# Two graph layers on Trainium2: bank reads of pass 2 ahead of other ready work, and the second tile's softmax and end placed half a pair later

## Chip, core and metric

The kernel runs on one core of one Trainium2 chip. The metric is the device time in microseconds (us) of the whole program. Everything is float32 on the way in and out.

## What is computed

Two layers over 128 graphs of 64 nodes with 768 features. Each layer normalizes its input, clips it at zero, computes a graph layer and adds it to its input. The first graph layer (pass 1 of the kernel) multiplies by three 768x768 weights and mixes by the adjacency. The second (pass 2) is a gated graph attention with six heads of 128. Cut to the second:

```python
def _L1_gnn_ref(feat_in, adj, W, b, w_src, w_dst, H_w, H_b):
    h = jnp.einsum('bni,hio->bhno', feat_in, W)
    th = jnp.tanh(h)
    attn_src = jnp.einsum('bhno,hoz->bhnz', th, w_src)
    attn_dst = jnp.einsum('bhno,hoz->bhnz', th, w_dst)
    attn = attn_src + jnp.swapaxes(attn_dst, -1, -2)
    attn = jnp.where(attn >= 0, attn, leaky_alpha * attn)
    attn = jnp.where(mask, NEG_MASK, attn)          # mask: adj == 0
    attn = jax.nn.softmax(attn, axis=-1)
    feat_out = jnp.einsum('bhnm,bhmo->bhno', attn, h) + b
    feat_out = jax.nn.elu(...)                       # heads side by side
    gate = jax.nn.sigmoid(feat_in @ H_w.T + H_b)
    return gate * feat_out + (1.0 - gate) * feat_in

h = jnp.maximum(_layernorm(x, axis=-1), 0.0)
x = x + _L1_gnn_ref(h, adj, ...)
```

## The kernel before

A tile is 128 rows, that is two graphs; a pair is two tiles; there are 32 pairs, and each pass goes through them. In pass 2 the input of a pair (256 x 768) times the two weights (features W and gate H_w, side by side) is computed by a fast matrix scheme: the operand is cut into 2 x 3 blocks, the weights into 3 x 3, and 15 products of sums of blocks (f1 to f11 of the input, g of the weights) give the six blocks of the output instead of 18. The products go into four named banks of PSUM, a (two buffers), b, c and d (one each). A product after the first in a bank is added to what the bank holds, and each time the bank is read, the reading is added to or taken from one block of the output. So the next product into a bank has to wait until the last one was read.

```python
PRODUCTS = (   # input sum, weight sum, bank, first in the bank, output block, sign, ...
    ("f1", "g6", "a", True, "11", "+", False),
    ("f7", "g10", "b", True, "00", "-", False),
    ("a01", "b11", "d", True, "01", "+", True),
    ("f4", "b21", "a", False, "01", "-", False),
    ("a00", "g12", "b", False, "01", "-", False),
    ("f3", "g8", "c", True, "12", "-", False),
    ("a02", "g14", "a", False, "00", "-", False),
    ("f9", "g9", "b", False, "02", "+", False),
    ("f11", "b10", "d", True, "00", "+", True),
    ("f6", "g5", "a", False, "02", "+", False),
    ("f8", "g3", "b", False, "12", "-", False),
    ("f10", "b12", "c", False, "02", "+", True),
    ("f5", "b22", "a", False, "12", "-", False),
    ("a11", "g1", "b", False, "11", "+", True),
    ("f2", "g11", "a", False, "10", "+", True),
)
```

The reading of a bank and the product (line numbers as in the profile: L736 and L738 add or take away, L741 to L748 are the first writes of a block):

```python
def read(b, c, sign, first, ss):
    # ... to: block c of the output, ps: the bank
    op = nc.vector.tensor_add if sign == "+" else nc.vector.tensor_sub
    if not first:
        if sign == "+":
            op(to, ps, to)                     # L736
        else:
            op(to, to, ps)                     # L738
        return
    if ss.start == 0:
        nc.scalar.activation(to[:, 0], ps[:, 0], AF.Copy,           # L741
                             scale=1.0 if sign == "+" else -1.0)
    if ss.stop == 2:
        s = 1 - ss.start
        if sign == "+":
            op(to[:, s], ps[:, s], hbb[:, cols])                    # L746
        else:
            op(to[:, s], hbb[:, cols], ps[:, s])                    # L748

def product(an, bn, b, first, c, sign, begins, ss):
    def step(q):
        # ...
        nc.tensor.matmul(bank[b][:, : n * CQ], OPS[p, an][:, q, :],     # L755
                         bw2[bn][:, ...], start=(first and q == 0), stop=(q == KQ - 1), ...)
        if q == KQ - 1:
            read(b, c, sign, begins, ss)
    for q in range(KQ):
        steps.append(lambda q=q: step(q))

for ss in ((slice(0, 2),) if p < NP - 1 else (slice(0, 1), slice(1, 2))):
    # ... 15 products each: 30 steps of 512 columns, in the last pair 60 of 256
```

Around these products lies the work of the tiles, by these functions (cut):

```python
heads(t)    # ScalarE tanh (L774), VectorE product with w_src and w_dst (L776),
            # 12 ScalarE sums over a head (L781, L783), GpSimd splits them in bf16 (L784 to L791)
swap(t)     # DMA: the two graphs of the tile change halves
gate(t)     # ScalarE tanh of the gate (L811)
rows(t)     # TensorE (L803), VectorE (L805), ScalarE (L807): row factors of the scores
softmax(t)  # TensorE scores (L819), VectorE masks (L821), ScalarE leaky (L823),
            # VectorE maximum (L825), 6 ScalarE exponentials (L829)
turn_p(t)   # 3 TensorE transposes (L840), ScalarE copy (L842)
attend(t)   # 12 TensorE products (L857), 6 VectorE operations (L861)
final(t)    # ScalarE exponential (L871), VectorE L872, L873, L874, GpSimd starts the output DMA
turn, form  # TensorE transposes of the next pair's input (L704), ScalarE copies (L709),
            # VectorE sums f1 to f11 (L241, L243)
```

For each pair the steps of the products are merged with side work: each entry is placed ahead of the product step of its number. The order in which the entries are written down is the priority; a scheduler then orders each engine's instructions by priority and readiness, once, when the program is built. Each engine runs its own list in order.

```python
def behind(p):      # the tiles of the pair before, beside the products of this one
    t0, t1 = 2 * p, 2 * p + 1
    return [(0, lambda: gate(t0)),
            (1, lambda: (heads(t1), swap(t1))),
            # ... see the diff
            (22, lambda: final(t1))]

def last():         # the last pair's own tiles, beside its own products
    return [(31, lambda: (heads(t1), swap(t1))),
            # ...
            (38, lambda: rows(t0)), (40, lambda: softmax(t0)),
            (46, lambda: rows(t1)), (48, lambda: softmax(t1)),
            (54, lambda: turn_p(t0)), (56, lambda: attend(t0)),
            (99, lambda: gate(t0)), ...]                     # the rest after the products

for p in range(NP):
    more = [(3, lambda: finish(NP - 1))] if p == 0 else []
    if p == NP - 1:
        more += last()
    merged(main(p), own(p) + before(p + 1) + behind(p - 1) + more)
```

Of the kernel before, what the change touches and what calls it, by code (L numbers as in the profile page):

```python
# [79 lines left out]
def kernel(  # L80
# [56 lines left out]
    NP = NT // 2  # L137
# [501 lines left out]
    with ExitStack() as px:  # L639
# [16 lines left out]
        def load_x(t):  # L656
            p, k = divmod(t, 2)
            HM[t] = work.tile([P, D], F32, name="x", bufs=2)
            nc.sync.dma_start(HM[t], HHD[p][k * P : (k + 1) * P, :])
# [58 lines left out]
        def main(p):  # L718

            bank = {}  # L720
            steps = []
            for k in range(2):
                t = 2 * p + k
                HS[t] = hzs[t % 4][:, 0, :].rearrange("p (h o) -> p h o", h=H)
                Z[t] = hzs[t % 4][:, 1, :]

            def read(b, c, sign, first, ss):

                k, q = int(c[0]), int(c[1])
                cols = slice(q * CQ, (q + 1) * CQ)  # L730
                to = hzs[(2 * p + k) % 4][:, ss, cols]
                ps = bank[b][:, : (ss.stop - ss.start) * CQ].rearrange("p (s n) -> p s n", n=CQ)
# [19 lines that stand above are left out]
                    if first and q == 0:  # L752
                        bank[b] = psm.tile([P, 512], F32, name=f"pm{b}", bufs=2 if b == "a" else 1)
                    n = ss.stop - ss.start
                    nc.tensor.matmul(  # L755
                        bank[b][:, : n * CQ], OPS[p, an][:, q, :],
                        bw2[bn][:, (2 * q + ss.start) * CQ : (2 * q + ss.stop) * CQ],
                        start=(first and q == 0), stop=(q == KQ - 1), skip_group_check=True)
                    if q == KQ - 1:
                        read(b, c, sign, begins, ss)  # L760
                for q in range(KQ):
                    steps.append(lambda q=q: step(q))

            for ss in ((slice(0, 2),) if p < NP - 1 else (slice(0, 1), slice(1, 2))):
                seen = set()
                for an, bn, b, first, c, sign, _ in PRODUCTS:
                    product(an, bn, b, first, c, sign, c not in seen, ss)
                    seen.add(c)
            return steps

        def heads(t):

            th = work.tile([P, H, DO], F32, name="th")
            nc.scalar.activation(th, HS[t], AF.Tanh)  # L774
            pr = work.tile([P, 2, H, DO], F32, name="pr")
            nc.vector.tensor_mul(pr, th[:, None].to_broadcast([P, 2, H, DO]),  # L776
                                 wsd.rearrange("p s (h o) -> p s h o", h=H))
            sd = small.tile([P, 2, H], F32, name="sd")
            sg = small.tile([P, 3, H], F32, name="sg")
            for h in range(H):  # L780
                nc.scalar.activation(pr[:, 1, h, :], pr[:, 1, h, :], AF.Copy, accum_out=sd[:, 1, h : h + 1])  # L781
            for h in range(H):
                nc.scalar.activation(pr[:, 0, h, :], pr[:, 0, h, :], AF.Copy, accum_out=sg[:, 2, h : h + 1])  # L783
            nc.gpsimd.tensor_mul(sg[:, :GT, :], sd[:, 1:2, :].to_broadcast([P, GT, H]),  # L784
                                 gm[:, :, None].to_broadcast([P, GT, H]))
            sb = sdb[t % 2]
            for i in range(NPART):
                q = sb[:, :, i * H : (i + 1) * H]
                nc.gpsimd.tensor_copy(q, sg)
                if i < NPART - 1:  # L790
                    nc.gpsimd.tensor_sub(sg, sg, q)  # L791

        def swap(t):

            hx = HX[t] = work.tile([P, H, DO], F32, name="hx")
            for g in range(GT):
                nc.sync.dma_start(hx[g * N : (g + 1) * N], HS[t][(1 - g) * N : (2 - g) * N])

        def rows(t):


            ps = pss.tile([P, 512], F32, name="ps")
            nc.tensor.matmul(ps[:NR, : N + P], sdb[t % 2].rearrange("p c v -> p (c v)")[:, :NR], idr,  # L803
                             start=True, stop=True)
            nc.vector.tensor_mul(rrow[t % 2][: 2 * HB],  # L805
                                 ps[: 2 * HB, None, :N].to_broadcast([2 * HB, H, N]), de[: 2 * HB])
            nc.scalar.copy(lrow[t % 2][2 * HB :], ps[2 * HB : NR, N : N + P])  # L807

        def gate(t):

            nc.scalar.activation(Z[t], Z[t], AF.Tanh, scale=0.5)  # L811

        def softmax(t):

            p, k = divmod(t, 2)
            a = work.tile([P, H, N], F32, name="a")
            nc.gpsimd.memset(a, NEG_MASK / LEAKY)
            pl = pss.tile([P, 512], F32, name="ps")[:, : H * N].rearrange("p (h n) -> p h n", h=H)
            nc.tensor.matmul(pl, lrow[t % 2], rrow[t % 2], start=True, stop=True)  # L819

            nc.vector.copy_predicated(a, AI[p][:, k, None, :].to_broadcast([P, H, N]), pl)  # L821
            al = work.tile([P, H, N], F32, name="al", bufs=1)
            nc.scalar.activation(al, a, AF.Prelu, alpha=LEAKY)  # L823
            mx = small.tile([P, H], F32, name="mx")
            nc.vector.tensor_reduce(mx, al, AX.X, OP.max, negate=True)  # L825
            pb = PB[t] = work.tile([P, H, N], F32, name="pb")
            dn = DN[t] = small.tile([P, H], F32, name="dn")
            for h in range(H):
                nc.scalar.activation(pb[:, h, :], al[:, h, :], AF.Exp, bias=mx[:, h : h + 1],  # L829
                                     accum_out=dn[:, h : h + 1])  # L830
            nc.vector.reciprocal(dn, dn)
# [3 lines left out]
        def turn_p(t):  # L835

            pt = PT[t] = work.tile([P, HH, P], F32, name="pT")
            ps = pss.tile([P, 512], F32, name="ps")[:, : HH * P].rearrange("p (a b) -> p a b", a=HH)
            for c in range(HH):
                nc.tensor.transpose(ps[:, c, :],  # L840
                                    PB[t][:, 2 * c : 2 * c + 2, :].rearrange("p h n -> p (h n)"), ident)
            nc.scalar.copy(pt, ps)  # L842
# [55 lines left out]
        def behind(p):  # L898

            if p < 0:  # L900
                return []
            t0, t1 = 2 * p, 2 * p + 1
            return [(0, lambda: gate(t0)),
                    (1, lambda: (heads(t1), swap(t1))),
                    (2, lambda: load_x(t0)),
                    (4, lambda: gate(t1)),
                    (4, lambda: rows(t0)),
                    (6, lambda: softmax(t0)),
                    (10, lambda: load_x(t1)),
                    (11, lambda: rows(t1)),  # L910
                    (13, lambda: softmax(t1)),
                    (12, lambda: turn_p(t0)),
                    (14, lambda: attend(t0)),
                    (15, lambda: final(t0)),
                    (19, lambda: turn_p(t1)),
                    (21, lambda: attend(t1)),
                    (22, lambda: final(t1))]

        def last():

# [23 lines left out]
# [5 lines that stand above are left out]
# [45 lines left out]
```

## Time and profile before

| | |
|---|---|
| time, median of 3 | 2579.61 us (2579.23 to 2581.2) |
| span of the profiled execution | 2577.0 us, TensorE clock granted 0.993 |
| pass 1 | up to about 1510 us |
| pass 2 | from there to the end |
| a pair in the middle of pass 2 (2001.80 to 2034.07 us) | 32.27 us |
| in it busy: TensorE, VectorE, ScalarE, GpSimd | 31.25, 26.58, 22.51, 7.45 us |

A row of the waits names the engine and line that waited, and the engine and line that ended the wait. In the timeline the columns are the start, the length, the engine, the line, the operation and what it writes and reads, and how many instructions stand together in the row; a wait ahead of it is in square brackets. A float32 product of the kernel appears as two records. The ends of matmuls are modelled, so the pace of TensorE is read from the starts.

### The profile page before, as it was taken

The page shows a single profiled execution, that of the slowest core. Times are in us where ns is not written, and L with a number is a line of the kernel's source. Part 1 is how long each engine was busy: PE and PEld are TensorE (multiplying, and loading weights), DVE is VectorE, ACT ScalarE, POOL GpSimd, SP SyncE. Part 2 cuts the span into 40 slices and gives each one's busy share as a digit, 9 for nine tenths or more (in the row PEclk, how much of TensorE's full clock was granted, in tenths as well). Part 3 has the DMA queues.
Part 4 walks back from the last instruction along what each step waited for, and adds up shares of the span by engine and source line. Part 5 has one row for each costly group of instructions (what it writes and reads, how often), then busy time and mean ns, then how long its engine had stood idle before and what let it go on. Part 6 is the DMA issues. An engine that isn't in the chain of part 4 may idle for free.

```text
span 2577.0 us, 35545 instructions
## 1 busy us (share of the span) xinstructions
PE 2489.3 (97%) x12072; PEld 1714.2 (67%) x12072; DVE 1980.3 (77%) x4130; ACT 1079.5 (42%) x3588; POOL 492.3 (19%) x801
## 2 busy tenths in 40 slices
PE   5999999999999999999999999999999999999996
PEld 4788888888888888888888864444444444444444
DVE  8977777777777777777777557888888888888887
ACT  1222222222222122222222216666666666666666
POOL 0121121211212112121121111222222222222222
PEclk8999999999999999999999999999999999999998
DMA  5122121221312212122121263444444444444433
GB/s 172 56 74 80 52 102 52 76 78 52 103 52 76 78 52 102 52 78 76 52 101 50 79 203 78 100 100 100 99 100 100 101 100 101 99 100 100 100 75 77
DMA packets 115047, 224.19 MB, mean 87 GB/s; under 512 B 36538, under 2 KB 48941, under 8 KB 114866
## 3 DMA queue, kind: packets, MB, share of 16 engines
q1 hardware_dynamic: 105208, 196.70, 23.3%
q0 software_dynamic: 9504, 25.17, 6.9%
q8 instruction: 95, 1.56, 0.3%
q14 instruction: 86, 0.70, 0.1%
q10 hardware_dynamic: 154, 0.06, 0.0%
HBM read 95.67 MB, written 100.66 MB: 76 GB/s over the span
## 4 chain that ended last, share of the span: by engine, by line
PE 71%; DVE 18%; ACT 6%; issue 4%; DMA 1%; POOL 1%; SPq 0%; POOLq 0%; DVEq 0%; ACTq 0%
PE pwa L544 19%; PE pwb L544 16%; PE pwc L544 6%; PE pma L755 6%; PE pwd L544 6%; PE pmb L755 6%; PE pb L497 5%; DVE f L861 3%; ACT pb L829 3%; DVE op L243 3%; PE pmc L755 2%; DVE pr L776 2%; DVE f L874 2%; DVE f L872 2%; DVE weights L738 1%
## 5 line engine op out<-in xcount | busy, mean ns | idle before, releaser
L544 PE MATMUL pwa<-weights,op 128*128 128x256 f32 x2304 | 542.6, 383 | 4.3 <-DVE x L536 3.1
L544 PEld LDWEIGHTS pwa<-weights,op 128*128 128x128 f32 x2304 | 423.0, 190 | 73.4 <-DVE x L536 12.0
L243 DVE TENSOR_TENSOR op<-op 128x768 f32<-128x768 f32 (+1 forms) x512 | 339.8, 683 | 156.4 <-ACT op L505 154.5
L505 ACT COPY op<-pb 128x768 f32<-128x768 f32 x160 | 124.2, 798 | 757.0 <-PE pb L497 757.0
L755 PE MATMUL pma<-weights,op 128*128 128x512 f32 (+1 forms) x792 | 381.5, 597 | 35.2 <-DVE weights L738 29.3
L544 PE MATMUL pwb<-weights,op 128*128 128x256 f32 x1536 | 372.2, 383 | 12.9 <-DVE x L538 9.5
L544 PEld LDWEIGHTS pwb<-weights,op 128*128 128x128 f32 x1536 | 285.9, 191 | 60.7 <-DVE x L538 10.3
L755 PE MATMUL pmb<-weights,op 128*128 128x512 f32 (+1 forms) x528 | 252.4, 591 | 3.6 <-DVE weights L738 3.5
L755 PEld LDWEIGHTS pma<-weights,op 128*128 128x128 f32 x792 | 137.8, 191 | 173.8 <-issue 96.4
L225 POOL TENSOR_TENSOR rn<-ve,mhalf 128x1 f32<-128x1 f32 x128 | 89.0, 695 | 530.5 <-DVE ve L224 526.9
L544 PE MATMUL pwc<-weights,op 128*128 128x256 f32 x768 | 184.9, 383 | 0.0
L544 PE MATMUL pwd<-weights,op 128*128 128x256 f32 x768 | 176.2, 379 | 0.0
L755 PEld LDWEIGHTS pmb<-weights,op 128*128 128x128 f32 x528 | 97.0, 193 | 118.4 <-issue 82.9
L218 DVE BATCH_NORM_STATS2 st<-x 128x6 f32<-128x384 f32 x256 | 136.4, 547 | 44.7 <-DMA x<-in_x_dram 43.5
L476 POOL COPY c<-cnt 128x243 bf16<-128x243 bf16 x64 | 46.2, 751 | 649.3 <-PE pb L484 602.3
L497 PE MATMUL pb<-r,h 64*128 64x192 f32 x1536 | 153.0, 339 | 7.8 <-ACT h L406 7.7
L544 PEld LDWEIGHTS pwc<-weights,op 128*128 128x128 f32 x768 | 143.2, 190 | 25.1 <-issue 7.0
L544 PEld LDWEIGHTS pwd<-weights,op 128*128 128x128 f32 x768 | 145.9, 190 | 19.8
L572 ACT ACTIVATE hf<-x,rn 128x768 f32<-128x768 f32 x64 | 65.8, 1028 | 213.7 <-DVE rn L226 213.7
L497 PEld LDWEIGHTS pb<-r,h 64*128 64x128 f32 x1536 | 124.6, 189 | 42.7 <-issue 30.5
L829 ACT ACTIVATE pb<-al,mx 128x64 f32<-128x64 f32 x384 | 128.3, 335 | 14.8 <-DVE mx L825 14.8
L574 POOL TENSOR_TENSOR x<-x,hf 128x768 f32<-128x768 f32 x64 | 115.9, 1812 | 85.4 <-ACT hf L572 85.4
(152 smaller groups left out, 4160.3 us busy)
## 6 DMA issues: line engine op xcount, KB each, us to landing
x<-in_x_dram SPq DMA_DIRECT2D x64, 384.0 KB
h<-hf SPq DMA_DIRECT2D x64, 384.0 KB
out_dram<-x SPq DMA_DIRECT2D x64, 384.0 KB
hh<-hh SPq DMA_DIRECT2D x64, 384.0 KB
h<-h SPq DMA_DIRECT2D x64, 384.0 KB
x<-hh SPq DMA_DIRECT2D x64, 384.0 KB
hx<-weights SPq DMA_DIRECT2D x128, 192.0 KB
out_dram<-f POOLq DMA_DIRECT2D x62, 384.0 KB, 4.9
```

The costliest lines, as they stand in the source:

```text
L218: ins = nc.vector.bn_stats(st[:, i, :], src[:, i * HALF : (i + 1) * HALF])
L225: nc.gpsimd.tensor_tensor(to[:, 0:1], ve, mhalf, op=OP.pow)
L243: return (nc.vector.tensor_add if s1 == "+" else nc.vector.tensor_sub)(to, x, y)
L497: nc.tensor.matmul(ps[:, g, i * 3 * N : (i + 1) * 3 * N], H0[t][s, kb * P : (kb + 1) * P], rts[p % 2][s, k].rearrange("p s n -> p (s n)"), ...
L505: nc.scalar.copy(a.rearrange("p h s (g n) -> p g (h s) n", g=GT), ps[:, :, : 6 * N].rearrange("p g (x n) -> p g x n", n=N))
L544: nc.tensor.matmul(bank[b][:, :CQ], OPS[p, an][:, q, s, :], bw[bn][:, (s * KQ + q) * CQ : (s * KQ + q + 1) * CQ], start=(first and q == s ...
L572: nc.scalar.activation(h, X[t], AF.Relu, scale=to[:, 0:1], bias=to[:, 1:2])
L574: nc.gpsimd.tensor_add(X[t], X[t], h)
L755: nc.tensor.matmul(bank[b][:, : n * CQ], OPS[p, an][:, q, :], bw2[bn][:, (2 * q + ss.start) * CQ : (2 * q + ss.stop) * CQ], start=(first a ...
L776: nc.vector.tensor_mul(pr, th[:, None].to_broadcast([P, 2, H, DO]), wsd.rearrange("p s (h o) -> p s h o", h=H))
L829: nc.scalar.activation(pb[:, h, :], al[:, h, :], AF.Exp, bias=mx[:, h : h + 1], accum_out=dn[:, h : h + 1])
L861: nc.vector.scalar_tensor_tensor(FF[t][:, h * DO : (h + 1) * DO], po[h % 2][:, h // 2, :], DN[t][:, h : h + 1], bb, op0=OP.mult, op1=OP.add)
```

## The change

Two things. First, the reads of pass 2's banks are put down under high priority, so that the scheduler takes a read that is ready before any other ready work of its engine. Second, the side work of the pair before is placed anew: the second tile's softmax, attention and end come some half a pair (about 15 steps) after the first tile's, instead of closely behind. Beside the last pair, which has 60 steps in place of 30, the numbers are doubled. What it is for: the next product into a bank shall not wait because its read stands behind end operations on VectorE, and the two tiles' work on VectorE and ScalarE shall be spread over the pair.

```diff
--- before.py
+++ after.py
@@ -757,7 +757,8 @@
                         bw2[bn][:, (2 * q + ss.start) * CQ : (2 * q + ss.stop) * CQ],
                         start=(first and q == 0), stop=(q == KQ - 1), skip_group_check=True)
                     if q == KQ - 1:
-                        read(b, c, sign, begins, ss)
+                        with tc.high_priority():
+                            read(b, c, sign, begins, ss)
                 for q in range(KQ):
                     steps.append(lambda q=q: step(q))
 
@@ -900,21 +901,23 @@
             if p < 0:
                 return []
             t0, t1 = 2 * p, 2 * p + 1
-            return [(0, lambda: gate(t0)),
-                    (1, lambda: (heads(t1), swap(t1))),
-                    (2, lambda: load_x(t0)),
-                    (4, lambda: gate(t1)),
-                    (4, lambda: rows(t0)),
-                    (6, lambda: softmax(t0)),
-                    (10, lambda: load_x(t1)),
-                    (11, lambda: rows(t1)),
-                    (13, lambda: softmax(t1)),
-                    (12, lambda: turn_p(t0)),
-                    (14, lambda: attend(t0)),
-                    (15, lambda: final(t0)),
-                    (19, lambda: turn_p(t1)),
-                    (21, lambda: attend(t1)),
-                    (22, lambda: final(t1))]
+            steps = [(0, lambda: gate(t0)),
+                     (2, lambda: load_x(t0)),
+                     (4, lambda: rows(t0)),
+                     (6, lambda: softmax(t0)),
+                     (6, lambda: (heads(t1), swap(t1))),
+                     (8, lambda: gate(t1)),
+                     (12, lambda: turn_p(t0)),
+                     (14, lambda: attend(t0)),
+                     (15, lambda: final(t0)),
+                     (15, lambda: load_x(t1)),
+                     (16, lambda: rows(t1)),
+                     (18, lambda: softmax(t1)),
+                     (24, lambda: turn_p(t1)),
+                     (26, lambda: attend(t1)),
+                     (27, lambda: final(t1))]
+
+            return [(2 * i, f) for i, f in steps] if p == NP - 2 else steps
 
         def last():
```

## Prediction

> **What bounds the kernel now.** I read the page's busy shares and slices first, to see how many stages there are, then the waits of TensorE alone, then one pair of tiles of pass 2 in the timeline, then the stretches of the tail.
>
> ```profile
> PE 2489.3 (97%) x12072; PEld 1714.2 (67%) x12072; DVE 1980.3 (77%) x4130; ACT 1079.5 (42%) x3588; POOL 492.3 (19%) x801
> PE   5999999999999999999999999999999999999996
> PEld 4788888888888888888888864444444444444444
> DVE  8977777777777777777777557888888888888887
> ACT  1222222222222122222222216666666666666666
> ```
>
> Two stages show. Up to about 1510 us is pass 1; from there pass 2, in which the weight loads fall from 8 to 4 tenths, VectorE rises to 8 and ScalarE to 6. Only pass 2 is touched by the change. TensorE is "busy" nearly everywhere, so what counts is who it waits for:
>
> ```profile
> PE pma L755 <- DVE weights L738: 29.3, 29, 1.0
> PE pwb L544 <- DVE x L538: 9.5, 2, 8.7
> PE pb L497 <- ACT h L406: 7.7, 1, 7.7
> PE pb L443 <- DVE ab L415: 4.5, 1, 4.5
> PE pmb L755 <- DVE weights L738: 3.5, 1, 3.5
> ```
>
> The columns are total us, number of waits, longest. One wait comes back 29 times, 1.0 us each: a product into bank a cannot start until VectorE has read that bank (line 738). Pass 2 has 32 pairs, so this is once in nearly every pair. The timeline of TensorE and then of VectorE around one of them:
>
> ```profile
> 1993.22 1.98 PE L755 MATMUL pma<-weights,op 128*128 128x512 f32 x4
> 1995.04 1.02 PE L755 MATMUL pmb<-weights,oq 128*128 128x512 f32 x2
> ...
> 1998.91 1.88 PE L755 MATMUL pmd<-weights,op 128*128 128x512 f32 x4
> 2001.80 0.70 PE L755 MATMUL pma<-weights,op 128*128 128x512 f32 x1 [1.01 <-DVE weights L738]
> ```
> ```profile
> 1995.80 1.74 DVE L776 TENSOR_TENSOR pr<-th,wsd 128x1536 f32<-128x1536 f32 x1
> 1997.46 0.95 DVE L872 SCALAR_TENSOR_TENSOR f<-e,f 128x768 f32<-128x768 f32 x1
> ...
> 1999.87 0.95 DVE L874 SCALAR_TENSOR_TENSOR f<-weights,f 128x768 f32<-128x768 f32 x1
> 2000.74 0.41 DVE L243 TENSOR_TENSOR op<-op 128x256 f32<-128x256 f32 x1
> 2001.07 0.68 DVE L738 TENSOR_TENSOR weights<-weights,pma 128x512 f32<-128x512 f32 x1
> ```
>
> The product f5·b22 leaves bank a at about 1995.04. Its read runs at 2001.07, six us later, because VectorE first does the score product (L776), the three end operations of the second tile (L872 to L874) and three sums of operands. TensorE fills in with the next pair's f1 and a01 products and then stands still for f2·g11. The pmd group starts at 1998.91; four records of 512 columns advance 1.72 us elsewhere (1995.04 to 1995.89 is two of them), so the next group could start at 2000.63 and starts at 2001.80: 1.17 us lost. The pair repeats every 32.27 us (2001.80 to 2034.07).
>
> How much of 32.27 us is work? By starts: 30 products of 0.86 us = 25.8; 12 transposes of the operands, 0.108 each = 1.3; 6 of the probabilities = 0.65; two groups of 12 small attention products, 0.89 each = 1.8; the row and score products of two tiles, about 0.5. Sum 30.1 us. So 2.2 us are lost: 1.17 in the bubble, about 1.0 in some ten places of 0.1 us, where a weight load is released just too late (after the copy of the probabilities, after each attention group, after row factors from GpSimd or ScalarE).
>
> **The Trainium skill.** "Perfetto Trace Analysis", section Identifying the Most-Contended Engine, says that matmul busy time is no measure of closeness to the limit and that weight-load busy time is better. The trace agrees: 97% busy, yet 2.2 of 32.27 us per pair (7%) can be won. The same page, section Optimization Strategy, says that a bubble that repeats on the engine that should be saturated can mean too few buffers. Here the trace shows another cause: the bank's reader is queued behind unrelated work. "PSUM — Partial Sum Buffer", section Engine vs sequencer instructions, says that VectorE's and ScalarE's queues are strictly first in, first out. The trace agrees: the L738 read could have run from 1995.04 but ran in its place in the order, after L874.
>
> **The change, part by part.** No instruction is added or removed; the counts per pair stay (80 on TensorE, 54 on VectorE, 60 on ScalarE). What moves is the order that the scheduler makes.
>
> 1. Reads first. In the changed order the f5 read stands directly behind L776 and ahead of the operand sums; no end operation stands between. I walk one pair with the durations above, with t = 0 at the end of f10·b12 (bank c). TensorE: four transposes 0.43, f5 to 2.15, a11 and three transposes to 4.2, next f1 (one half) to 5.06, attention to 5.95; there f2 wants bank a. VectorE: read of bank c to 0.73, maximum 0.46, two sums 0.66 to 1.86, L776 1.68 to 3.54, the f5 read 0.60 to 4.15. It is done 1.8 us before f2 wants it: the 1.17 us go.
>
> 2. The second tile half a pair later. The end of tile 1 (L872 to L874, 2.6 us) now falls beside f6, f3 and f10 in the middle of the pair, where I find bank reads with slack: f6's bank b is read at 2.45 us after attention and wanted at 4.83. Exponentials and copies of the two tiles no longer meet: the waits of 0.1 us for the second tile's row factors and for lrow should mostly vanish (now 2 per pair, 0.2 us).
>
> 3. Where new waits may stand. (a) Attention of tile 1 needs: read of bank c 0.75, tanh 0.8, six exponentials 6 x 0.35 = 2.1, gate tanh 0.76, copy 0.46 = 4.95 with hand-overs 5.0 to 5.1, and TensorE arrives at 5.06: no slack. (b) After it ScalarE has 12 sums of 0.295 = 3.5 (to 8.45), copy of bank a 0.27, tanh 0.76, copy 0.28, exponential 0.85, gate 0.76, copy of bank b 0.28, to 11.7; VectorE then runs L776 (9.6 to 11.28), L872 to 12.15 and the f7 read to 12.56; TensorE wants bank b for a00 at 12.2 plus its own small losses of some 0.3: between 0 and 0.35 us of wait. (c) The row factors of tile 0 come from GpSimd at about 10.2 against 10.35. I charge 0.1 to 0.4 us per pair for these, less the 0.2 of point 2: net 0.2 us, 6 us in all.
>
> The pair becomes 32.27 - 1.17 + 0.2 = 31.3 us. For 29 pairs: 29 x 0.97 = 28 us.
>
> 4. The last pair. It runs in halves of 256 columns (60 steps), and the side steps of the pair before are now stretched over all of it.
>
> ```profile
> 2513.76:2559.62 45.86, 38.31 (x214) 27.60 (x213) 37.29 (x78) 34.56 (x167) 11.13 (x29) 0.93 0.39 85
> 2559.62:2577.00 17.38, 1.72 (x27) 1.06 (x27) 8.24 (x22) 3.98 (x10) 3.50 (x4) 0.62 0.39 45
> ```
>
> Columns: stretch and length, then busy time with count of TensorE, weight loads, VectorE, ScalarE, GpSimd, then clock and DMA. From the first half-width product to the last one 45.9 us for some 27 us of TensorE work, with waits of 3.5 and 2.5 us on bank reads; then 17.4 us of end. The same walk through the changed order gives about 37 us for the first stretch (what is left is waits of up to 1.7 us for row factors), 9 us less. But three tiles' softmax then stand behind the last product, where before most of it lay beside the waits: row factors and first maximum 2.35, three rounds of six exponentials with their hand-overs to 11.0, two exponentials and the copy to 12.75, attention to 13.75, the last end in halves to 18.2, against 8.8 us before (2559.6 to 2568.4); the 8.6 us of output and close stay. That is 9 us more. Net 0, give or take 4.
>
> Pass 1 and the first pair (a wait of 3.4 us for L746) keep their work; I count 0 to -1 us. Sum: 2579.6 - 28 = 2552 us.
>
> **Rivals.** (A) The bubble moves: the period is set by ScalarE (22.5 of 32.27 us busy) and VectorE (26.6) in their queues, and a wait of (a) or (b) takes the place of the L738 wait. For it: VectorE at 82% with items of 1.7 us ahead of reads, and chains without slack. Against: no chain that I walked is over by more than 0.4 us. Then 2560 to 2570. (B) The small losses go as well, since reads come early and weight loads are released in time: 1.5 us per pair, 2535 to 2542. Against: those after attention and the probability copy stay where they were. (C) The tail grows: three softmaxes at the end in series, with the stretch before them not shortened. Then up to 9 us is given back: 2561. (D) Priority of reads delays operand sums (L243) so that products wait for operands. The four transposes and sums of the next pair stay ahead of use by a whole product each, so I give this little.
>
> **Range and chances.** 2552 us; 8 in 10 between 2541 and 2566: the lower end is (B) in part, the upper is (A) or (C). 2% would be 2528 us, 52 us less; even all 2.2 us of 30 pairs is 66, so this needs nearly every loss to go: 0.03. Slower by 2% would need 1.6 us more per pair than now: 0.02. Within 2%: 0.95.
>
> **What would show it.** Right: the L738 wait of 29 x 1.0 gone from the waits of TensorE; the period near 31.3 us; the f5 read within 2.2 us after its product; stretches of 37 and 26 us in the tail. Wrong: a repeated wait of about 1 us with another name (copy of the probabilities, row factors, L748), or a period under 31, or a last pair and end together far from 63 us.

## The result and the profile after

The changed kernel takes 2591.19 us (median of 4 runs, 2589.06 to 2593.83) against 2580.26 us: a ratio of 1.0043, 95% interval 1.0026 to 1.006. It is a little slower; 2552 us was predicted. In the profiled executions the span grew by 10.3 us, from 2577.0 to 2587.3.

The page's busy shares, and TensorE's waits (engine and line that waited, who ended it, total us, times, longest). Lines from L776 of the kernel before on have moved by one: L777 is the score product, L790 and L792 GpSimd's splitting, L804 the row product.

```profile
PE 2469.7 (95%) x12072; PEld 1718.4 (66%) x12072; DVE 1994.6 (77%) x4130; ACT 1070.9 (41%) x3588; POOL 514.3 (20%) x801
```
```profile
PE ps L804 <- POOL sdb L790: 57.1, 31, 2.1
PE pwb L544 <- DVE x L538: 9.5, 2, 8.7
```

The wait for the read of bank a (L738, 29.3 us in 29 waits) is gone. A new one stands first: the row product of a tile waits for its operands from GpSimd, 31 times, 57.1 us. GpSimd's own busy time rose by 22 us (492.3 to 514.3) with 801 instructions in both kernels: the same work took longer. (The total alone is a weak sign: with the reads' precedence alone, below, it is 486.4 us beside a wait of 44.0 us.) Three timelines of the changed kernel over the same few microseconds show it: TensorE, GpSimd, VectorE (start, length, engine, line, operation; in brackets the wait ahead of it).

```profile
2003.19 1.45 PE L755 MATMUL pma<-weights,op 128*128 128x512 f32 x3
2004.48 1.88 PE L755 MATMUL pmb<-weights,op 128*128 128x512 f32 x4
2008.21 0.28 PE L804 MATMUL ps<-idr,sdb 128*82 128x192 bf16 x1 [1.85 <-POOL sdb L790]
```
```profile
2004.39 0.20 POOL L790 CAST sdb<-sg 128x18 bf16<-128x18 f32 x1 [1.59 <-issue]
2004.67 0.22 POOL L792 TENSOR_TENSOR sg<-sg,sdb 128x18 f32<-128x18 f32 x1
2004.96 0.43 POOL L790 CAST sdb<-sg 128x18 bf16<-128x18 f32 x1
2005.46 1.82 POOL L792 TENSOR_TENSOR sg<-sg,sdb 128x18 f32<-128x18 f32 x1
2007.35 0.80 POOL L790 CAST sdb<-sg 128x18 bf16<-128x18 f32 x1
```
```profile
2005.45 1.76 DVE L777 TENSOR_TENSOR pr<-th,wsd 128x1536 f32<-128x1536 f32 x1
2007.12 0.97 DVE L873 SCALAR_TENSOR_TENSOR f<-e,f 128x768 f32<-128x768 f32 x1
```

GpSimd's five small operations start at 2004.39 and end at 2008.15, 3.8 us. The fourth, 0.22 us elsewhere, takes 1.82 us and ends with VectorE's score product of the other tile; the fifth takes 0.80 us and ends with L873, which reads two SBUF tiles as well. TensorE was ready at 2006.36. The pair is 32.39 us (2001.80 to 2034.19) against 32.27. In terms of the pair: 32.27 - 1.17 (bubble gone) - 0.56 (the rest, by difference; not traced to single waits) + 1.85 (new wait) = 32.39.

The last pair, in two stretches as before (columns as there):

```profile
2518.40:2552.60 34.20, 31.18 (x181) 24.62 (x180) 27.94 (x59) 26.04 (x128) 9.38 (x27) 1.00 0.25 58
2552.60:2587.30 34.70, 8.97 (x87) 5.58 (x85) 18.21 (x45) 13.52 (x50) 4.76 (x6) 0.56 0.42 69
```

It starts 4.6 us later than before (2518.4 against 2513.8), and its two stretches take 68.9 us instead of 63.2: the other 5.7 us. The products end sooner, after 34.2 us; the end doubles from 17.4 to 34.7 us.

**Theories.** T1: GpSimd is held up while VectorE runs an operation with two operands in SBUF. T2: the sums simply come too late for the place where the row product stands in TensorE's order, whatever VectorE does. For the last pair: the precedence, the places or the doubling bunches the attention of the last three tiles behind the products.

### The profile page after: what moved, and what is told of

Read it like the earlier page. It is cut to its first block, busy times and chain, and to the rows that moved or that the text cites. A ratio compares the mean times of both kernels' runs of the same rounds, so it can differ in the third digit from the quotient of the medians.

```text
span 2587.3 us, 35433 instructions
## 1 busy us (share of the span) xinstructions
PE 2469.7 (95%) x12072; PEld 1718.4 (66%) x12072; DVE 1994.6 (77%) x4130; ACT 1070.9 (41%) x3588; POOL 514.3 (20%) x801
## 4 chain that ended last, share of the span: by engine, by line
PE 71%; DVE 14%; issue 5%; POOL 5%; ACT 4%; DMA 1%; SPq 0%; POOLq 0%; DVEq 0%; ACTq 0%
PE pwa L544 19%; PE pwb L544 16%; PE pwc L544 6%; PE pwd L544 6%; PE pb L497 5%; PE pmb L755 5%; PE pma L755 4%; PE pmd L755 3%; DVE op L243 3%; POOL sg L792 2%; ACT pr L782 2%; PE pmc L755 2%; DVE pr L777 2%; POOL sdb L790 2%; DVE weights L736 2%
## 5 line engine op out<-in xcount | busy, mean ns | idle before, releaser
L243 DVE TENSOR_TENSOR op<-op 128x768 f32<-128x768 f32 (+1 forms) x512 | 336.3, 681 | 156.1 <-ACT op L505 153.3
L755 PE MATMUL pma<-weights,op 128*128 128x512 f32 (+1 forms) x792 | 373.7, 587 | 3.2 <-DVE weights L746 3.2
L544 PEld LDWEIGHTS pwb<-weights,op 128*128 128x128 f32 x1536 | 285.9, 191 | 60.4 <-DVE x L538 10.3
L876 POOL DMA_DIRECT2D out_dram<-f x66 | 58.4, 890 | 388.6 <-DVE f L875 385.4
```

The costliest lines, as they stand in the source:

```text
L243: return (nc.vector.tensor_add if s1 == "+" else nc.vector.tensor_sub)(to, x, y)
L544: nc.tensor.matmul(bank[b][:, :CQ], OPS[p, an][:, q, s, :], bw[bn][:, (s * KQ + q) * CQ : (s * KQ + q + 1) * CQ], start=(first and q == s ...
L876: nc.gpsimd.dma_start(of[t * P : (t + 1) * P, c], f, accum_op=OP.add)
```

## Experiments

Where an experiment says that the order is kept, each engine's list was recorded from the changed kernel and laid down by edges without semaphores, so that the scheduler cannot answer an edit with another order (cut):

```python
for order in recorded.values():                 # one list of instructions per engine
    for prev, name in zip(order, order[1:]):
        tc.add_manual_dep(traced[name], prev, DependencyInfo(NoSync, DATA), reason="pinned order")
```

All ratios are against the kernel before, run on the same chip.

### The score product reads PSUM

This leaves out the distinct score vectors of the heads and of source and target, so its output differs; the number and size of the operations stay.

```diff
+        wps = psk.tile([P, 512], F32, name="wps")       # in PSUM
+        nc.vector.tensor_copy(wps, wsd[:, 0, :512])
-            nc.vector.tensor_mul(pr, th[:, None]..., wsd.rearrange("p s (h o) -> p s h o", h=H))
+            nc.vector.tensor_mul(pr, th[:, None]..., wps[:, None, None, :DO].to_broadcast([P, 2, H, DO]))
```

> Every engine keeps the changed kernel's order; only the score product's second operand (VectorE, 128x1536) comes from PSUM instead of SBUF, holding one 64-wide vector for all heads, so the six separate score vectors and the source/target difference are left out. Theory 1, GpSimd is held up while VectorE reads two SBUF operands: the last subtraction before the row operands falls from 1.82 us to about 0.2-0.3 us, TensorE's wait of the row product for the GpSimd operands falls from 57 us in all to under 6 us, the pair goes from 32.4 to about 30.6-31.2 us and the time to 2535-2557 us. Theory 2, the sums simply come too late for where the row product stands in TensorE's order: the subtraction may change, the wait stays above 35 us, and the time stays at 2580-2592 us.

(The vector in PSUM is 128 wide, as the code has it.) 2541.63 us, ratio 0.985 (0.9833 to 0.9866). The pair is 30.88 us (2010.88 to 2041.76 between the same GpSimd operation), the wait at the row product 2.4 us in all. GpSimd and VectorE of this run at the same place of the pair (L880 and L878 are the splitting, L865 the score product):

```profile
2013.30 0.36 POOL L878 CAST sdb<-sg 128x18 bf16<-128x18 f32 x1
2013.74 0.22 POOL L880 TENSOR_TENSOR sg<-sg,sdb 128x18 f32<-128x18 f32 x1
2014.03 0.20 POOL L878 CAST sdb<-sg 128x18 bf16<-128x18 f32 x1
```
```profile
2013.72 1.75 DVE L865 TENSOR_TENSOR pr<-th,wps 128x1536 f32<-128x1536 f32 x1
```

VectorE's product is as long as ever, 1.75 us, and starts just as the subtraction does; the subtraction takes 0.22 us in its midst. Order, sums and places are those of the changed kernel, so T2 alone is out: with nothing moved, the wait fell from 57.1 to 2.4 us. The edit also makes the second operand one vector that repeats; the version with tanh in PSUM below has the PSUM operand without that, with the same effect.

### The ports by themselves

Not part of the model; a GpSimd chain of 18-column operations beside three VectorE operations of 1536 columns.

```python
for beside in (none, two_sbuf, one_psum, single, stt) * 3:
    nc.scalar.copy(st, pr); nc.scalar.copy(st[:, :18], q)       # common start
    for _ in range(3): beside()
    nc.gpsimd.tensor_copy(sg, st[:, :18])
    for _ in range(6):
        nc.gpsimd.tensor_copy(q, sg); nc.gpsimd.tensor_sub(sg, sg, q)
```

> No part of the model: three rounds of five cases, in each of which GpSimd runs 13 operations on 18 columns in a row while VectorE runs three operations on 1536 columns behind the same start: none; product of two SBUF tiles; product of an SBUF tile and a PSUM tile; one SBUF tile plus a constant; (tile times constant) minus a second SBUF tile. If GpSimd is held up whenever VectorE reads two SBUF operands: 0.20-0.22 us an operation beside nothing and beside the PSUM product, and in the second and fifth case about one GpSimd operation per VectorE operation stretched to 1.5-2 us, so that those chains last about 5 us longer. If any large VectorE operation does it: the PSUM and the one-operand case are stretched too.

The first GpSimd operations beside two SBUF operands (VectorE from 13.20 to 18.54), then beside SBUF and PSUM (from 21.43), then beside one SBUF operand and a constant (from 28.64), in the timeline of this run:

```profile
13.31 1.71 POOL L165 COPY sg<-st 128x18 f32<-128x18 f32 x1
15.09 1.73 POOL L167 CAST q<-sg 128x18 bf16<-128x18 f32 x1
16.89 1.74 POOL L168 TENSOR_TENSOR sg<-sg,q 128x18 f32<-128x18 f32 x1
18.69 0.20 POOL L167 CAST q<-sg 128x18 bf16<-128x18 f32 x1
...
21.53 0.20 POOL L165 COPY sg<-st 128x18 f32<-128x18 f32 x1
21.79 0.20 POOL L167 CAST q<-sg 128x18 bf16<-128x18 f32 x1
22.07 0.22 POOL L168 TENSOR_TENSOR sg<-sg,q 128x18 f32<-128x18 f32 x1
...
28.74 0.92 POOL L165 COPY sg<-st 128x18 f32<-128x18 f32 x1 [3.62 <-ACT st L162]
29.73 0.93 POOL L167 CAST q<-sg 128x18 bf16<-128x18 f32 x1
30.73 0.94 POOL L168 TENSOR_TENSOR sg<-sg,q 128x18 f32<-128x18 f32 x1
```

In this run one GpSimd operation gets through for each VectorE operation with two SBUF operands, and it lasts until that one ends. Spans on GpSimd are rough, but the starts say the same: 1.78 and 1.80 us apart, 0.26 to 0.28 us beside the PSUM product. The operation with a tile, a constant and a second SBUF tile holds as well (1.72 to 1.74 us). The one-operand case went against the expectation: it holds GpSimd for its own shorter length. "SBUF — State Buffer" in the Trainium skill, section Who interferes with whom, says all three: two SBUF inputs contend with GpSimd's reads; at most one does not; and `tensor_scalar` can run in a mode that takes the pair of ports that GpSimd shares. This run agrees, with the sizes above; that the one-operand case ran in such a mode is not shown by it.

### The row product two half-products later

Nothing is left out. The changed kernel's order up to the last pairs, with one instruction of TensorE moved from ahead of the two half-products of bank d to behind them: in 27 pairs by the trace. In the two pairs before the last it stands in its old place and still waits 1.85 us.

> The changed kernel with one instruction moved on TensorE in each of 29 pairs: the row product of the first tile comes two half-products later, some 3 us. Both theories: the subtraction stays at about 1.8 us. If the wait is only one of place, it falls from 1.85 us a pair to 0-0.3 us; the next limit may be a product bank's read (0.3-0.5 us). Pair about 30.8-31.3 us, time 2540-2560 us. If the wait only passes on to the next instruction that needs the attention chain (logits, transposes), the pair stays at 32 us or more and the time above 2575 us.

2551.59 us, ratio 0.9889 (0.9874 to 0.9904); pair 30.92 us where it was moved, wait at the row product 9.0 us in six waits. The subtraction still took 1.82 us: the hold is there, and nearly nobody waits for it. So the loss needs both: a chain that is held, and a consumer within reach of it. T2 has this much truth.

### Each part alone

```diff
 reads only: the kernel before, and
-                        read(b, c, sign, begins, ss)
+                        with tc.high_priority():
+                            read(b, c, sign, begins, ss)
 places only: the changed kernel with this undone
```

> The kernel before with the precedence of the reads alone, the softmax steps in their old places. The wait of the second product for its bank (29.3 us in all) goes. Theory 1 and 2 alike: the steps of the second tile's sums stay at their old place (1), so whether a new wait appears depends on where the score product and the row product land; if none does, 2545-2560 us; if the row product waits for GpSimd as in the changed kernel, 2580-2592 us.

> The changed kernel's places without the precedence of reads. If the places alone cause the new wait, TensorE waits 40-60 us in all at the row product for the GpSimd operands, and the time is 2580-2610 us, the bank wait of the kernel before partly on top. If the new wait needs both parts, it stays under 10 us and the time is near before's plus the longer tail, 2575-2590 us.

| | old places | new places |
|---|---|---|
| reads in their turn | 2580.73 us, pair 32.27 | 2557.9 us, pair 31.48 |
| reads first | 2591.19 us, pair 32.50 | 2591.19 us, pair 32.39 |

(Pairs from the profiles. Three of the times are from one chip; that of both together is the result above, against 2580.26 us.) Reads alone: ratio 1.0044 (1.0029 to 1.0059); places alone: 0.9913 (0.9898 to 0.9928). The reads alone fell where their expectation put them if the row product waits; the places alone came out below both of theirs. Either part alone ends the repeated wait for L738: no such wait is left with the reads alone, one of 1.5 us with the places alone. TensorE's first waits, reads only and then places only:

```profile
PE ps L804 <- POOL sdb L790: 44.0, 32, 2.3
```
```profile
PE ps L803 <- POOL sdb L789: 26.2, 30, 1.7
```

Why did the row product not wait before? There GpSimd is held as well, beside operand sums of VectorE (L243). The end of one chain in the kernel before, and the row product that uses it:

```profile
2003.10 0.99 POOL L791 TENSOR_TENSOR sg<-sg,sdb 128x18 f32<-128x18 f32 x1
2004.16 0.20 POOL L789 CAST sdb<-sg 128x18 bf16<-128x18 f32 x1
2005.34 0.25 PE L803 MATMUL ps<-idr,sdb 128*82 128x192 bf16 x1
```

The operands are ready at 2004.36 and TensorE comes at 2005.34: 0.98 us to spare, behind a bubble of 1.17 us at 2001.80. Without the bubble alone some 0.2 us of wait would be left. With the reads alone it is 1.36 us:

```profile
2011.18 1.75 DVE L777 TENSOR_TENSOR pr<-th,wsd 128x1536 f32<-128x1536 f32 x1
2011.40 1.61 POOL L792 TENSOR_TENSOR sg<-sg,sdb 128x18 f32<-128x18 f32 x1
2014.05 0.28 PE L804 MATMUL ps<-idr,sdb 128*82 128x192 bf16 x1 [1.36 <-POOL sdb L790]
```

The same four products stand ahead of the row product. Counted from the start of the first of them (1997.19 before, 2005.65 here), TensorE comes 1.11 us sooner (7.04 us against 8.15) and the operands 1.17 us later (8.34 against 7.17). The bubble hid about half of it. The other half is a chain that the new order delays: one subtraction now stands beside the score product and is held for 1.61 us.

In the places-only run the score product starts (2022.45) 1.20 us after the chain instead of 1.06, and one more of the five operations gets through ahead of it: one operation is held long (1.61 us), not two, and the wait is 0.84 us instead of 1.85.

```profile
2021.25 0.20 POOL L789 CAST sdb<-sg 128x18 bf16<-128x18 f32 x1 [1.59 <-issue]
...
2021.89 0.36 POOL L789 CAST sdb<-sg 128x18 bf16<-128x18 f32 x1
2022.33 0.28 POOL L791 TENSOR_TENSOR sg<-sg,sdb 128x18 f32<-128x18 f32 x1
2022.67 1.61 POOL L789 CAST sdb<-sg 128x18 bf16<-128x18 f32 x1
```

### The move in the list of steps, and without precedence

```diff
-                     (4, lambda: rows(t0)),
-                     (6, lambda: softmax(t0)),
+                     (8, lambda: rows(t0)),            # second run: 6, and no precedence of reads
+                     (10, lambda: softmax(t0)),        # second run: 8
```

> The plain form of the move of the row product: its step in the list from 4 to 8, the first tile's softmax from 6 to 10; everything else as in the changed kernel. TensorE's wait at the row product falls from 57 us to under 12 us in all (GpSimd's own stretch may stay), the pair from 32.4 to 30.8-31.3 us, the time to 2545-2562 us with the long tail still in it. If some later step of the first tile then waits instead (logits, transposes): above 2575 us.

> The changed kernel without the reads' precedence, with the first tile's rows at 6 and softmax at 8. Scheduled order puts the row product behind both half-products of bank d. Wait at the row product under 5 us in all, no bank wait above 0.3 us a pair, pair 30.8-31.2 us, tail like that of the kernel with the places alone (61 us): 2537-2550 us. If the reads without precedence come late again: a wait at bank a or b of 0.5-1.2 us a pair and 2555-2575 us.

2567.88 us, ratio 0.996 (0.9946 to 0.9975), and 2578.0 us, ratio 1.0 (0.9991 to 1.0009). Both missed their expectations. Moving an entry moves more than one instruction: in the first run the sums and the row product came later together, the subtraction still took 1.61 us and TensorE still waited 0.70 us in a pair (20.6 us in 28 waits). In the second the wait at the row product nearly went (2.6 us), and the old one for L738 came back in every second pair (18.0 us in 14 waits); its last pair takes 77 us. These runs say little of the cause, and much of the lever: a step number is a poor handle for one instruction's place.

### The last pair

```diff
 no doubling: the changed kernel with
-            return [(2 * i, f) for i, f in steps] if p == NP - 2 else steps
+            return steps
 no precedence in the last pair: the run with the row product moved, its end scheduled anew, with
-                        with tc.high_priority():
+                        with tc.high_priority() if p < NP - 1 else ExitStack():
 old places: that, and for p == NP - 2 the steps of the kernel before (doubled)
```

> The changed kernel without the doubling of the positions for the pair before the last. Steady pairs unchanged (32.4 us, last pair's first product at about 2518 us). If the doubling is what makes three tiles' attention stand in a row behind the last product: product stretch 34 to 38-42 us, end 34.7 to 18-24 us, the sum 69 to 58-64 us and the time 2580-2587 us. If the end comes of the last pair's own list: sum and time unchanged within 2 us.

> The run with the row product moved by two half-products, but reads take precedence only up to the last pair but one; the last pair's end is scheduled without it. Steady part as there (last pair's first product at about 2480 us). If precedence pushes the attention of the last three tiles behind the last product: products 36 to 38-46 us, end 34.7 to 17-27 us, the sum 70.6 to 60-65 us and the time to 2540-2547 us. If the bunching comes from the places: sum 69-72 us, time 2549-2554 us.

> As the run before, and the pair before the last also has the old places of the steps (still doubled as in the changed kernel's rule). If the places cause the bunching: sum 60-64 us and 2540-2546 us whatever the run before shows; if neither does: sum 68-72 us, 2549-2554 us.

| kernel | products + end, us | sum | time, us | ratio (95%) |
|---|---|---|---|---|
| before | 45.9 + 17.4 | 63.2 | | |
| changed | 34.2 + 34.7 | 68.9 | 2591.19 | 1.0043 (1.0026 to 1.006) |
| reads only | 31.3 + 29.1 | 60.5 | 2591.19 | 1.0044 (1.0029 to 1.0059) |
| places only | 33.4 + 28.5 | 61.9 | 2557.9 | 0.9913 (0.9898 to 0.9928) |
| no doubling | 35.9 + 35.0 | 70.9 | 2594.53 | 1.0071 (1.0054 to 1.0089) |
| row product moved | 35.9 + 34.7 | 70.6 | 2551.59 | 0.9889 (0.9874 to 0.9904) |
| ... no precedence in the last pair | 35.8 + 28.4 | 64.1 | 2544.06 | 0.9864 (0.9849 to 0.9879) |
| ... and old places there | 45.3 + 16.1 | 61.4 | 2541.48 | 0.9855 (0.984 to 0.987) |

The doubling is not what lengthens the end; without it the sum is 2 us longer. Precedence and places lengthen it together: each alone gives 60.5 to 61.9 us, both 68.9. Taking the precedence out of the last pair gives back 6.5 us, old places 2.7 more. The row products of the last three tiles tell part of it. In the kernel before, and then in the changed kernel:

```profile
2530.88 0.28 PE L803 MATMUL ps<-idr,sdb 128*82 128x192 bf16 x1 [0.17 <-POOL sdb L789]
2544.29 0.28 PE L803 MATMUL ps<-idr,sdb 128*82 128x192 bf16 x1
2552.05 0.37 PE L803 MATMUL ps<-idr,sdb 128*82 128x192 bf16 x1
```
```profile
2548.46 0.28 PE L804 MATMUL ps<-idr,sdb 128*82 128x192 bf16 x1 [1.95 <-POOL sdb L790]
2552.65 0.25 PE L804 MATMUL ps<-idr,sdb 128*82 128x192 bf16 x1
2554.91 0.25 PE L804 MATMUL ps<-idr,sdb 128*82 128x192 bf16 x1
```

Before, the three tiles' attention starts over 21 us, all three ahead of the last product's end (2559.6). Changed, all three start within 6.5 us around the last products, and run behind one another with TensorE nearly idle (9.0 us busy of 34.7). Bunching by itself is not the difference, though: with the places alone the three start within 3.5 us (2520.73 to 2524.26), but the last of them 1.1 us ahead of the products' end (2525.4), where in the changed kernel it comes 2.3 us behind it. And in the changed kernel VectorE's part of the last tile's attention waits once more:

```profile
2574.40 1.64 DVE L862 SCALAR_TENSOR_TENSOR f<-ps,dn,bb 128x128 f32<-128x128 f32 x6 [2.23 <-DMA out_dram<-f]
```

The tile f has two buffers, and the last tile's is free only when an earlier output has landed. Such a wait stands in no trace of the kernel before, of either part alone, or of the two runs without precedence in the last pair. By sums, 3.4 + 2.2 us make up most of the 6.2 us by which the end is longer than with the places alone (34.7 against 28.5), but no run takes the two apart. Nor is the buffer needed for a long end: without the doubling no such wait is seen and the end takes 35.0 us; there the last two row products come 6.6 and 8.3 us behind the products. Why the two settings together place the last tiles so late stays open.

### A version that beats both

Nothing is left out here: four of the six tanh heads go to a free PSUM bank, the score product is made in two operations, and the changed kernel's order is kept.

```diff
-            th = work.tile([P, H, DO], F32, name="th")
-            nc.scalar.activation(th, HS[t], AF.Tanh)
+            th = psk.tile([P, 4, DO], F32, name="th")                  # PSUM
+            tl = work.tile([P, 2, DO], F32, name="tl")
+            nc.scalar.activation(th, HS[t][:, :4], AF.Tanh)
+            nc.scalar.activation(tl, HS[t][:, 4:], AF.Tanh)
-            nc.vector.tensor_mul(pr, th[:, None]..., wsd...)
+            nc.vector.tensor_mul(pr[:, :, :4], th[:, None]..., wv[:, :, :4])
+            nc.vector.tensor_mul(pr[:, :, 4:], tl[:, None]..., wv[:, :, 4:])
```

> Nothing left out. The changed kernel's order on every engine, but the score product reads four of the six tanh heads from PSUM (128x1024 in one operation, about 1.2 us) and only the last two from SBUF (128x512, about 0.6 us), in two operations in that order; ScalarE writes tanh in two pieces. If two SBUF operands are what holds GpSimd up, the subtraction that took 1.82 us takes 0.2-0.7 us, the wait at the row product falls from 57 us to under 10 us in all, the pair to 30.8-31.2 us, the time to 2538-2550 us. If not: wait above 35 us, time above 2578 us.

2539.36 us, ratio 0.9848 (0.9832 to 0.9865); pair 30.79 us, wait at the row product 2.2 us. GpSimd and VectorE:

```profile
2011.76 0.22 POOL L797 TENSOR_TENSOR sg<-sg,sdb 128x18 f32<-128x18 f32 x1
2012.05 0.20 POOL L795 CAST sdb<-sg 128x18 bf16<-128x18 f32 x1
```
```profile
2011.54 1.22 DVE L782 TENSOR_TENSOR pr<-th,wsd 128x1024 f32<-128x1024 f32 x1
2012.68 0.68 DVE L783 TENSOR_TENSOR pr<-tl,wsd 128x512 f32<-128x512 f32 x1
```

The part that holds GpSimd, the last two heads, starts after the chain has ended. With the end of the program without precedence and with old places:

> Nothing left out. The steady part of the run with four tanh heads in PSUM (last pair's first product at about 2470 us there) and the end of the run with old places and no precedence in the last pair (59-63 us from there). If the two gains are independent they add: 2539.4 us less some 8 to 10 us, 2528-2534 us. If the end was good only behind that steady part: 2535-2541 us.

2535.58 us, ratio 0.9835 (0.9818 to 0.9851): the lowest of all, though its interval overlaps that of the version above. It lies at the second of its expectations: of the 8 to 10 us 3.8 came. The traces don't put this down to the end: the last pair and the end take 60.9 us there, against 68.1 us above, so 7.2 us came. But the last pair's first product starts 5.5 us later (2473.6 against 2468.1), of which 4.0 us are there before the first pair's product of bank c (1532.0 against 1528.0), 2.0 of them before pass 2's first product. Why is open.

## Why the prediction was wrong

**Step 1 was right.** The L738 wait is gone and the bubble with it. The precedence removes it, as the walk has it (the run with the reads alone has no such wait); the run with the places alone shows that it wasn't needed for that.

**Step 2 is not shown.** It took 0.2 us in a pair off for smaller losses; by difference 0.56 us went, but which waits these were was not measured.

**Step 3 failed, at (c).** In its clock (f2 starts at 5.95, at 2001.80 in the trace, so t = 0 is 1995.85) the sums of ScalarE were to end at 8.45 and ended at 8.4 (2004.28 by ScalarE's timeline); the score product was to run from 9.6 to 11.28 and ran from 9.6 to 11.4; the row product wanted its operands at 10.35 and was ready at 10.5. Only the step between was off: GpSimd's chain was to deliver at 10.2 and delivered at 12.3. It was charged at about its length beside nothing (1.75 us from the end of the sums; it took 3.9 us), while the same paragraph had VectorE in a two-operand product from 9.6 on. The margin of 0.15 us was also counted as no cost. The 0.1 to 0.4 us a pair charged for new waits became 1.85 us. A repeated wait for row factors was among the signs of being wrong that the prediction named. Points (a) and (b) held: no repeated wait for the copy of the probabilities, and one wait of 0.3 us for L748. (The terms of (a) add up to 4.87, not 4.95; it changes nothing here.)

The pair without this wait is 30.8 to 30.9 us in three kernels, better than the 31.3 that the prediction gave; rival (B) is part of the truth. Had the chain not been held, the predicted 2552 us would have been 10 us too high (2541.63 us measured).

**Step 4 failed in its end.** The product stretch was near (34.2 against 37), the end was not (34.7 against 26). With t = 0 at the last product's end (2552.6), the first maximum was to end at 2.35 and ended at 2.4, the last exponentials at 11.0 and 12.7. From there it came apart: the copy of the last probabilities at 12.75 and 16.3, the last attention at 13.75 and 18.0, the last end operation at 18.2 and 26.6; the 8.6 us of output and close took 8.1. The walk had no wait between the tiles' ends: TensorE's last transposes waited 2.51 us for VectorE (L862 of the tile before), and VectorE 2.23 us for the output DMA shown above.

```profile
2567.51 0.87 PE L841 MATMUL ps<-ident,pb 128*128 128x128 f32 x3 [2.51 <-DVE f L862]
```

**Rivals.** (A) came true in that the bubble moved, but through (c) and an engine that it didn't name: GpSimd, 20% busy. (C) came true with 5.7 us. Together they turned a gain of 28 us into a loss of 10.

## What to carry to other kernels

Before a bubble is removed, look at what stood behind it with less slack than the bubble is long: here 0.98 us behind 1.17. Then look at whether the new order delays that chain too: by 1.17 us in the run with the reads alone. When a short GpSimd chain feeds the critical engine, look at what VectorE does in the same microsecond; a small operation whose maximum is eight times its median is a sign of being held, and one operand in PSUM frees it without making VectorE slower. Test a priority and a placement apart before joining them: the places alone gained 0.9%, the precedence alone lost 0.4%, and both together lost 0.4% as well.

## What was not expected of the hardware

By the run with the ports alone, a GpSimd operation of 0.2 us lasts until the end of the VectorE operation beside it when that one reads two SBUF tiles: 1.71 to 1.74 us beside 1.76 us, one GpSimd operation for each VectorE operation in a row of three. It does not always get through after one: in the kernel before, the operation below lasts past the ends of L243 (1999.95) and L874 (2000.82), until the next L243 ends (2001.15).

```profile
1999.59 1.63 POOL L784 TENSOR_TENSOR sg<-sd,gm 128x12 f32<-128x12 f32 x1 [5.61 <-ACT pr L781]
```

A VectorE operation with a single SBUF operand and a constant (0.96 us for 128x1536) holds it too, for 0.92 to 0.94 us. With the second operand in PSUM VectorE takes the same 1.75 us and GpSimd its 0.20 to 0.22.
